# Turning the neighbour mask of a graph network: TensorE transposes replaced by DMA transposes, and 22 masks split 11 and 11 instead of 14 and 8

## The chip, the cores and the metric

The kernel runs on one core of a Trainium2 chip. Its time is the device time of one execution in microseconds, as the median of several runs. Beside it there is one execution recorded by the profiler, and all durations of single instructions come from that one.

## The reference

A graph has N = 2708 nodes with D = 512 numbers each and an adjacency matrix `adj` of N x N integers (0 or 1, some 2.4% ones, the diagonal all ones). Four layers follow each other, each with a residual sum and a layer norm. Only the first uses a limited mask: of each row's neighbours it keeps the first 64.

```python
def _L0_gnn_ref(X, A, W_nb, b_nb, W_line, b_line, neibor_num):
    Ab = A > 0
    keep = Ab & (jnp.cumsum(Ab.astype(jnp.int32), axis=1) <= neibor_num)
    cnt = keep.sum(axis=1, keepdims=True).astype(X.dtype)
    nb_sum = keep.astype(X.dtype) @ X
    nb_mean = nb_sum / jnp.maximum(cnt, 1.0)
    xj = jax.nn.leaky_relu(nb_mean @ W_nb.T + b_nb)
    xi = jax.nn.leaky_relu(X @ W_line.T + b_line)
    return xi + jnp.where(cnt > 0, xj, jnp.zeros((), X.dtype))
...
x = _layernorm(x + _L0_gnn_ref(x, adj, L0_gnn_W_nb, L0_gnn_b_nb, L0_gnn_W_line, L0_gnn_b_line, 64), axis=-1)
x = _layernorm(x + _L1_gnn_ref(x, adj, ...), axis=-1)
x = _layernorm(x + _L2_gnn_ref(x, adj, L2_gnn_W, L2_gnn_a), axis=-1)
x = _layernorm(x + _L3_gnn_ref(x, adj, ...), axis=-1)
```

Layer 1 averages over all neighbours, layers 2 and 3 are graph attention with the same adjacency as a mask.

## The kernel before

The rows are cut into NT = 22 tiles of P = 128 (the last has 20 rows, `few`). TensorE contracts over the partitions, so each aggregation over neighbours needs the mask with its *columns* on the partitions: `maskT` (L82) is 128 x 22 x 2816 in fp8; `maskT[p, j, i]` tells of node i and its neighbour j x 128 + p. It stays in SBUF for all four layers. It holds three values: a neighbour that is kept is negative, one beyond the 64th positive, no neighbour is zero. What comes after the first layer takes the sign off.

**How one mask (one tile of 128 rows of `adj`) is made.**

1. `load_mask` (L270) brings 128 x 2708 integers from memory as bf16 on POOL's DMA queue.
2. `count` (L275): ScalarE turns it into exact 0 and 1 (Sigmoid with a huge scale) and sums each row into `cnts`.
3. `place` (L279): DVE runs a scan along the row (L283), a running sum from -64.5, capped at 0.5, then multiplies the mask by it (L286). A neighbour thus gets its negative place or a positive half. A row is done in 2 parts in the first stage and in 4 among the sums.
4. `turn` (L288): TensorE transposes 22 blocks of 128 x 128 in bf16 (L295) into PSUM, in three groups of at most G = 8; after each group ScalarE takes the Sign from PSUM to `maskT` (L299), which also changes bf16 to fp8. After the last group a small DMA on POOL's queue (L302) copies the 20 rows of the last block to partitions 32 to 51 (`TWIN`), where the low half of y's last tile lies.

The masks are made in the order `turns` (L268): the short cut of tiles 20 and 21 first, so mask 1 is the one with 20 rows.

**First stage** (L331 to L358), one pass over the 22 row tiles. Each row t has two products of 512 x 512 on TensorE: y = x W_nb^T (L335) and xi = x W_line^T (L350). `transposed` (L129) turns x by TensorE (L133), and ScalarE copies it out of PSUM (`xT`, L135). `keep_y` (L230) keeps y in two parts, the rounded `yH` on ScalarE (L231) and the remainder `yL` on DVE (L236). DVE adds the bias and applies the leaky relu (L352, L195), and POOL's queue stores xi to `r0_dram` (L354). Rows of x are loaded two ahead on SP's queue (`fetched`, L171), into three row buffers. In this pass HERE = NT - 8 = 14 masks are made, one at a row where the condition in L343 holds: two out of three rows or more, from row 2 on. A mask is loaded one mask ahead (`early(1, ...)`, L326, three buffers `m`). At its row it is counted after `yH` (L346), placed in two parts after `yL` and after the leaky relu (L348, L356), and turned about one row later (L339).

The order on an engine is largely the order in which the code issues; `pe` (L104) chains TensorE's instructions one after another by hand, and `tc.issue_after` holds an instruction behind a named one.

**Sums** (L483 to L510). Six cuts of up to four row tiles, the short one first. For each j of 22 column tiles, ScalarE makes `kT` (L369), the kept mask as 0 or 1 in fp32r, from `maskT`, one step ahead, and TensorE does 8 matmuls of 128 x 512 (4 tiles, `yH` and `yL`) into four PSUM banks (L496). At the end of a cut ScalarE evicts the four sums (L509). At each j the loop also advances a generator `both` by one step (L502): first `other_masks` (L372), which makes the other 8 masks, one each 11 steps or so, in time for their cut; then `weights1` and `vectors`, which prepare the weights of later layers. Another generator, `todo`, advanced two times out of three, is `finish` (L410): the last cut's leaky relu, residual sum and layer norm on DVE, and its store on POOL's queue. The mask's buffers there are `room(i)` (L374), two of them by turns; the transposes use the PSUM tiles `pm0`, `pm1` (L397). `weight2` (L211) holds W_line in the first stage and again a weight from `weights1` on; in between it is not used.

What follows (L515 on) is layer 1's products, its aggregation over `maskT` and the attention layers, 2445 of the 2924 us. It is the same in both kernels.

Of the kernel before, what the change touches and what calls it, by code (L numbers as in the profile page):

```python
# [11 lines left out]
BF16 = mybir.dt.bfloat16  # L12
F8 = mybir.dt.float8e4
AF = mybir.ActivationFunctionType
# [4 lines left out]
P = 128  # L19
# [7 lines left out]
STEP = 2.0 ** 68  # L27
# [3 lines left out]
def kernel(  # L31
# [9 lines left out]
    nc = tc.nc  # L41
    N = x.shape[0]
    NT = -(-N // P)
    FULL = N // P
# [5 lines left out]
    def rows(t):  # L50
        return min(P, N - t * P)
# [11 lines left out]
    identb = const.tile([P, P], BF16, name="identb")  # L63
    nc.vector.tensor_copy(identb, ident)
    G = 8
# [16 lines left out]
    maskT = big.tile([P, NT, NT * P], F8, name="maskT")  # L82
# [12 lines left out]
    few = N - (NT - 1) * P  # L95
    LAST, TWIN = NT - 1, 32
# [61 lines left out]
    def early(first, n, make):  # L158

        made = {}  # L160

        def get(i, **how):
            for j in range(len(made), min(i + first + 1, n)):
                made[j] = make(j, **how)
            return made[i]
        return get
# [36 lines left out]
    with ExitStack() as phase:  # L203
        yp = phase.enter_context(tc.tile_pool(name="y", bufs=1))
        cnts = yp.tile([P, NT], F32, name="cnts")
# [56 lines left out]

        HERE = NT - 8
        cuts = [(b, min(b + 4, NT)) for b in range(0, NT, 4)]
        cuts = cuts[-1:] + cuts[:-1]
        turns = [t for b in cuts for t in range(*b)]  # L268

        def load_mask(i, m):  # L270
            n = rows(turns[i])
            nc.gpsimd.dma_start(m[:n], adj[turns[i] * P:turns[i] * P + n, :], max_dma_last_dim=N * 2)
            return m

        def count(i, m):  # L275
            t, n = turns[i], rows(turns[i])
            nc.scalar.activation(m[:n], m[:n], AF.Sigmoid, bias=gate[:n], scale=STEP, accum_out=cnts[:n, t:t + 1])

        def place(i, m, places, part, of):  # L279

# [4 lines left out]
                                         OP.add, OP.min)  # L285
            return nc.vector.tensor_mul(m[:n, c0:c1], m[:n, c0:c1], places[:n, :c1 - c0])  # L286

        def turn(i, m, psum, order=as_it_comes):  # L288
            t, n = turns[i], rows(turns[i])
            for g0 in range(0, NT, G):  # L290
                g1 = min(g0 + G, NT)
                ps = psum()
                for j in range(g0, g1):
                    w = rows(j)
                    order(nc.tensor.transpose(ps[:w, j - g0, :n], m[:n, j * P:j * P + w], identb[:n, :n]))  # L295
                parts = [(P, g0, min(g1, FULL))] + ([(rows(FULL), FULL, NT)] if g1 > FULL else [])
                for w, a, b in parts:
                    if a < b:
                        nc.scalar.activation(maskT[:w, a:b, t * P:t * P + n], ps[:w, a - g0:b - g0, :n], AF.Sign,  # L299
                                             saturate=False)  # L300
                if g1 == NT:
                    nc.gpsimd.dma_start(maskT[TWIN:TWIN + few, LAST, t * P:t * P + n],  # L302
                                        maskT[:few, LAST, t * P:t * P + n])
                yield

        def rows_of(src):
            return early(2, NT, lambda t: fetched(src, t, rows(t)))

        with ExitStack() as ph:
            st = ph.enter_context(tc.tile_pool(name="l0a", bufs=1))  # L310
            wnT, wlT = weight(), weight2
            room = [maskT[:, G + k, :4 * D].bitcast(F32) for k in range(2 * KD)]

            xs = rows_of(x)
            xTs = early(0, NT, lambda t, order=as_it_comes: transposed(ahead, ps_tr, xs(t), rows(t), "xT", order))

            transpose_weight(room[:KD], ps_tr, wnT, l0_w_nb, (nc.sync, nc.scalar))
            lows = {}  # L320
            for t in range(2):
                xT = xTs(t, order=pe)
                lows[t] = keep_y(t, P, product(xT, P, wnT, 0, pe))
            transpose_weight(room[KD:], ps_tr, wlT, l0_w_line)
            b_line = bias(bcast(l0_b_line, D))
            masks = early(1, HERE, lambda i: load_mask(i, st.tile([P, N], BF16, name="m", bufs=3)))  # L326
            masks(0)
            nc.gpsimd.memset(maskT[:, NT - 1, :], 0.0)
            nc.gpsimd.memset(maskT[:, :, N:], 0.0)
            counted = turned = 0  # L330
            for t in range(NT):  # L331
                n = rows(t)
                if t > 1:

                    lows[t] = keep_y(t, n, product(xTs(t, order=pe), n, wnT, 0, pe, sums() if t % 2 else None))  # L335
                xT = xTs(t)
                if t + 1 < NT:
                    xTs(t + 1, order=pe)
                while turned < counted - (t + 2 < NT):  # L339
                    for _ in turn(turned, masks(turned), lambda: sums(BF16, (P, G, P)), pe):  # L340
                        pass
                    turned += 1
                now = counted < min(HERE, -(-(t - 1) * HERE // (NT - 5)))  # L343
                if now:
                    m, places = masks(counted), st.tile([P, N // 2], BF16, name="places", bufs=1)
                    with tc.issue_after(highs[t].ins):  # L346
                        count(counted, m)
                    with tc.issue_after(lows[t].ins):  # L348
                        place(counted, m, places, 0, 2)
                pm = product(xT, n, wlT, 1, pe)  # L350
                u = sm.tile([P, D], F32, name="u")
                nc.vector.tensor_add(u[:n], pm[:n], b_line[:n])  # L352
                low = rows_made = leaky(u[:n], u[:n])
                nc.gpsimd.dma_start(r0_dram[t * P:t * P + n, :], u[:n])  # L354
                if now:
                    with tc.issue_after(low.ins):  # L356
                        place(counted, m, places, 1, 2)
                    counted += 1  # L358
# [3 lines left out]
        with ExitStack() as ph:  # L362
# [9 lines left out]
            def other_masks():  # L372

                def room(i):  # L374
                    r = (ahead.tile([P, 2 * KD * (D + 2 * H)], BF16, name="w", tag="w", bufs=1) if i % 2 else
                         st.tile([P, 2 * KD * D], BF16, name="spare", tag="spare"))
                    m = r[:, :N]
                    load_mask(i, m)
                    return m, r[:, N:N + N // 4 + 1]

                got = {HERE: room(HERE)}
                for i in range(HERE, NT):
                    if i + 1 < NT:
                        got[i + 1] = room(i + 1)
                    m, places = got.pop(i)
                    if i == HERE:
                        for _ in range(5):
                            yield
                    count(i, m)
                    yield  # L390
                    yield
                    for part in range(4):
                        place(i, m, places, part, 4)
                        yield
                    yield
                    yield
                    psum = (ps_mm.tile([P, G, P], BF16, name=f"pm{k % 2}") for k in range(3))  # L397
                    for _ in turn(i, m, lambda: next(psum)):
                        yield
                nc.vector.tensor_scalar(iso, cnts, 0.5, None, op0=OP.is_lt)  # L400
                nc.vector.tensor_scalar(rdeg, cnts, 1.0, None, op0=OP.max)
                nc.vector.reciprocal(rdeg, rdeg)
# [83 lines left out]
            for i, b in enumerate(cuts):  # L486
                ts_ = range(*b)
                pa = {t: sums() for t in ts_}
                for j in range(NT):
                    if j + 1 < NT:  # L490
                        nxt, nxt_made = kept(b, j + 1)
                    elif i + 1 < len(cuts):
                        nxt, nxt_made = kept(cuts[i + 1], 0)
                    for t in ts_:
                        for y in halves(j):
                            nc.tensor.matmul(pa[t], kT[:, (t - b[0]) * P:(t - b[0] + 1) * P], y[:, j, :],  # L496
                                             start=(j == 0 and y is yH), stop=(j == LAST))
                    kT = nxt
                    if j % 3:
                        next(todo, None)  # L500
                    with tc.issue_after(nxt_made.ins):
                        next(both, None)  # L502
                with tc.issue_after(nxt_made.ins):
                    reciprocals(slice(*b))
                us = {}
                for t in ts_:
                    n = rows(t)
                    us[t] = st.tile([P, D], F32, name=f"u{t - b[0]}")
                    nc.scalar.activation(us[t][:n], pa[t][:n], AF.Copy, scale=rkeep[:n, t:t + 1])  # L509
                todo = finish(ts_, us)  # L510
# [6 lines left out]
            for t in range(NT):  # L517
                n = rows(t)
# [989 lines left out]
```

## Time and profile before

| | us |
|---|---|
| runs | 2923.65, 2928.71, 2920.36 |
| median | 2923.65 |
| profiled execution, its own time | 2926.44 |
| its span, first to last instruction | 2924.5 |
| first stage and what lies ahead of it, to the first matmul of the sums | 202.5 |
| sums, to the last eviction | 276.7 |
| all the rest | 2445.3 |

Over the whole span TensorE is busy 2842.8 us (97%), its weight loads 1584.3, DVE 1983.5 (68%), ScalarE 1499.8 (51%), POOL 244.8 (8%). By stage:

| stretch | length | TensorE | DVE | ScalarE | POOL | share of the DMA engines |
|---|---|---|---|---|---|---|
| to the first sum | 202.5 | 187.7 | 152.8 | 95.9 | 36.6 | 0.50 |
| sums | 276.7 | 269.8 | 162.4 | 136.7 | 33.9 | 0.39 |
| rest | 2445.3 | 2385.3 | 1668.2 | 1267.2 | 174.3 | 0.17 |

The table's shares are means over a stretch; the engine that decides can change inside it. Matmuls are pipelined, so TensorE's busy time includes time in which one waits in the pipe.

In the groups of the profile a line reads: source line, engine, operation, output <- input by the program's names, shape and type, count; then busy time and mean ns of one, and the engine's idle time before such an instruction with what ended it. In a timeline a line begins with the start and the duration in us. In the list of DMA issues the numbers are the count, the KB of each and the median time from issue to landing.

### The profile page before, as it was taken

The page shows a single profiled execution, that of the slowest core. Times are in us where ns is not written, and L with a number is a line of the kernel's source. Part 1 is how long each engine was busy: PE and PEld are TensorE (multiplying, and loading weights), DVE is VectorE, ACT ScalarE, POOL GpSimd, SP SyncE. Part 2 cuts the span into 40 slices and gives each one's busy share as a digit, 9 for nine tenths or more (in the row PEclk, how much of TensorE's full clock was granted, in tenths as well). Part 3 has the DMA queues.
Part 4 walks back from the last instruction along what each step waited for, and adds up shares of the span by engine and source line. Part 5 has one row for each costly group of instructions (what it writes and reads, how often), then busy time and mean ns, then how long its engine had stood idle before and what let it go on. Part 6 is the DMA issues. An engine that isn't in the chain of part 4 may idle for free. (4 is left out here: it accounts for less than half of the span.)

```text
span 2924.5 us, 36470 instructions
## 1 busy us (share of the span) xinstructions
PE 2842.8 (97%) x14370; PEld 1584.3 (54%) x14370; DVE 1983.5 (68%) x2341; ACT 1499.8 (51%) x1749; POOL 244.8 (8%) x387
## 2 busy tenths in 40 slices
PE   8999999999999999999999999999999999999997
PEld 4557766458888333444466443444375555555555
DVE  6866637542334999999978999999954435435342
ACT  3546532112322999999965999999951000000001
POOL 1111101101110000000012000000200010100000
PEclk9999999999999999999999999999999999999999
DMA  5633426322222111111143111110161000000000
GB/s 130 131 88 72 109 80 184 123 63 91 83 72 78 33 37 36 35 45 39 38 142 122 37 37 36 45 51 34 35 160 60 4 26 15 26 15 16 15 22 21
DMA packets 122518, 181.58 MB, mean 62 GB/s; under 512 B 43007, under 2 KB 67908, under 8 KB 122338
## 3 DMA queue, kind: packets, MB, share of 16 engines
q1 hardware_dynamic: 92470, 117.50, 13.5%
q0 software_dynamic: 18864, 57.45, 6.9%
q10 hardware_dynamic: 11004, 4.22, 0.6%
q8 instruction: 115, 1.88, 0.3%
q14 instruction: 65, 0.53, 0.1%
HBM read 148.91 MB, written 44.65 MB: 66 GB/s over the span
## 5 line engine op out<-in xcount | busy, mean ns | idle before, releaser
L752 DVE SCALAR_TENSOR_TENSOR e<-v_bc,ucol,maskT 128x1408 f32<-128x1408 f32 (+3 forms) x804 | 1133.7, 1477 | 322.3 <-PE pn L1135 312.8
L781 ACT ACTIVATE c<-e,bcol 128x1300 fp8e4<-128x1300 f32 (+2 forms) x688 | 956.6, 1412 | 63.4 <-DVE e L752 18.6
L953 PE MATMUL po<-e,R 128*64 128x512 f32 (+3 forms) x4224 | 894.7, 548 | 26.3 <-DVE e L752 24.3
L953 PEld LDWEIGHTS po<-e,R 128*64 128x64 f32 (+1 forms) x4224 | 333.4, 136 | 554.7 <-issue 390.4
L1135 PE MATMUL pn<-e,R 128*128 128x512 f32 (+3 forms) x1056 | 403.0, 545 | 1.1 <-DVE lin L1155 0.3
L1135 PEld LDWEIGHTS pn<-e,R 128*128 128x128 f32 (+1 forms) x1056 | 183.9, 190 | 197.1 <-issue 181.5
L1085 ACT ACTIVATE w<-pl,b 128x256 f32<-128x256 f32 (+1 forms) x88 | 40.9, 465 | 371.0 <-PE pl L1083 371.0
L496 PE MATMUL acc<-yH,kT 128*128 128x512 f32 x484 | 195.2, 409 | 4.7 <-ACT kT L369 4.5
L547 PE MATMUL acc<-yH,mf 128*128 128x512 f32 x484 | 185.0, 389 | 0.0
L496 PE MATMUL acc<-yL,kT 128*128 128x512 f32 x462 | 180.8, 391 | 0.0
L547 PE MATMUL acc<-yL,mf 128*128 128x512 f32 x462 | 179.7, 389 | 0.0
L122 POOL TENSOR_TENSOR ln_rs<-ln_rs,half 128x1 f32<-128x1 f32 (+1 forms) x88 | 53.0, 602 | 1397.7 <-DVE ln_rs L121 1348.4
L674 PE MATMUL pm<-w,xT 128*128 128x264 f32 (+1 forms) x704 | 165.1, 387 | 3.4 <-ACT xT L135 1.6
L259 PE MATMUL pm<-weight,xT 128*128 128x512 f32 (+1 forms) x344 | 158.4, 604 | 8.2 <-DVE u L352 6.8
L1083 PE MATMUL pl<-lin 128*128 128x256 f32 (+1 forms) x704 | 155.9, 376 | 3.4 <-DVE lin L982 3.4
L1108 PE MATMUL pl<-lin,w 128*128 128x512 f32 x336 | 150.8, 593 | 0.0
L1083 PEld LDWEIGHTS pl<-lin 128*128 128x128 f32 x704 | 131.2, 193 | 34.5 <-issue 15.8
L674 PEld LDWEIGHTS pm<-w,xT 128*128 128x128 f32 (+1 forms) x704 | 129.7, 190 | 25.8 <-ACT xT L135 3.6
L544 ACT CAST mf<-maskT 128x1024 fp32r<-128x1024 fp8e4 (+1 forms) x66 | 64.5, 978 | 151.7 <-PE acc L547 148.1
L259 PE MATMUL pm<-w,xT 128*128 128x512 f32 x296 | 133.6, 594 | 5.8 <-ACT xT L135 2.1
L369 ACT ACTIVATE kT<-maskT 128x512 fp32r<-128x512 fp8e4 (+1 forms) x132 | 77.5, 594 | 115.6 <-PE acc L496 114.4
L853 PE MATMUL pd<-c,parts_c 128*12 128x384 fp8e4 (+2 forms) x2688 | 128.3, 307 | 0.0
(251 smaller groups left out, 2656.2 us busy)
## 6 DMA issues: line engine op xcount, KB each, us to landing
rows<-x_dram SPq DMA_DIRECT2D x63, 256.0 KB
v_bc<-v_dram SPq DMA_DIRECT2D x16, 704.0 KB
rows<-in_x_dram SPq DMA_DIRECT2D x42, 256.0 KB
x_dram<-u POOLq DMA_DIRECT2D x42, 256.0 KB, 2.5
v_bc<-v_dram SPq DMA_DIRECT2D x16, 650.0 KB
m<-in_adj_dram POOLq DMA_DIRECT2D x13, 677.0 KB, 6.9
r_dram<-u POOLq DMA_DIRECT2D x21, 256.0 KB, 2.3
rows<-r_dram SPq DMA_DIRECT2D x21, 256.0 KB
```

The lines of the kernel that those rows point to most:

```text
L259: order(nc.tensor.matmul(pm[:m], xT[:, k, :m], w[:, k, :], start=(k == 0), stop=(k == KD - 1)))
L369: made = nc.scalar.activation(kT[:, :w], maskT[:, j, b[0] * P:b[0] * P + w], AF.Relu, scale=-1.0)
L496: nc.tensor.matmul(pa[t], kT[:, (t - b[0]) * P:(t - b[0] + 1) * P], y[:, j, :], start=(j == 0 and y is yH), stop=(j == LAST))
L547: nc.tensor.matmul(pa, mf[:, j - g0, :], y[:, j, :], start=(j == 0 and y is yH), stop=(j == LAST))
L674: nc.tensor.matmul(pm[a][:m, :D // 2 + heads], xT[:, k, :m], w[:, k, a, :D // 2 + heads], start=(k == 0), stop=(k == KD - 1))
L752: self.made = nc.vector.scalar_tensor_tensor(e[:, :w], v[:, :w], ucol[:, j, h:h + 1], maskT[:, j, c0:c0 + w], op0=OP.max, op1=OP.mult)
L781: nc.scalar.activation(c[:, :w], e[:, :w], AF.Sigmoid, bias=bcol[:, j, h:h + 1], scale=STEP, saturate=False)
L853: pe(nc.tensor.matmul(p[32 * g:32 * g + 12, :c1 - c0], parts_c[:, j, h, :], c[:, c0:c1], start=(i == 0 and h == hs[0]), stop=(i == NT - 1 ...
L953: pe(nc.tensor.matmul(po[i][HO * k:HO * k + HO, :c1 - c0], R2[at, j, h * HO:(h + 1) * HO], e[at, a:a + c1 - c0], start=(i_ == 0), stop=(i_ ...
L1083: nc.tensor.matmul(pl[:, :w], self.lin1[:, k, f * P:(f + 1) * P], h[:, k, :w], start=(k == 0), stop=(k == KD - 1))
L1108: nc.tensor.matmul(pl[:n], gT[:, f, (t - t0) * P:(t - t0) * P + n], self.lin2[:, f, :], start=(f == 0), stop=(f == KF - 1))
L1135: nc.tensor.matmul(pn[k][:, :w], R2[at, j, k * P:(k + 1) * P], e[at, :w], start=(j == 0), stop=(j == NT - 1))
```

## The change

It does four things.

- **The turn.** The 22 TensorE transposes of a mask are replaced by one DMA transpose of the whole tile, 128 x 2816 in bf16, issued on SP's queue (`nc.sync.dma_start_transpose`). It writes 22 blocks of 128 x 128 into a buffer `into` in SBUF. A new generator `signs` does what ScalarE did before, from `into` instead of PSUM: Signs of 8, 8 and 5 blocks and of the 20 rows of the last block, then the small copy on POOL's queue.
- **Where the turned mask lands.** In the first stage there are four slots `idle`, pairs of column tiles of `maskT` whose own masks are not made yet, seen as bf16, taken by turns. Among the sums there is one buffer, `weight2` seen as bf16.
- **Its input.** The mask tiles are widened from 2708 to 2816 columns, and POOL zeroes the 108 spare ones before each load (the whole tile for the short mask).
- **The split.** HERE is NT - 11: eleven masks in the first stage, eleven among the sums. There `both` is advanced four steps for each three j, `signs` of the last mask runs between the parts of the next one's `place`, and the steps after a turn are three.

In the first stage, the Signs of a mask are issued just ahead of the next mask's transpose, about one row and a half after its own.

```diff
-        HERE = NT - 8
+        HERE = NT - 11
...
-            nc.gpsimd.dma_start(m[:n], adj[turns[i] * P:turns[i] * P + n, :], max_dma_last_dim=N * 2)
+            nc.gpsimd.dma_start(m[:n, :N], adj[turns[i] * P:turns[i] * P + n, :], max_dma_last_dim=N * 2)
...
-        def turn(i, m, psum, order=as_it_comes):
+        def turn(i, m, into):
+            nc.sync.dma_start_transpose(into, m)
+
+        def signs(i, into):
             t, n = turns[i], rows(turns[i])
-            for g0 in range(0, NT, G):
-                g1 = min(g0 + G, NT)
-                ps = psum()
-                for j in range(g0, g1):
-                    w = rows(j)
-                    order(nc.tensor.transpose(ps[:w, j - g0, :n], m[:n, j * P:j * P + w], identb[:n, :n]))
...
+            for w, a, b in [(P, a, min(a + G, FULL)) for a in range(0, FULL, G)] + [(few, FULL, NT)]:
+                nc.scalar.activation(maskT[:w, a:b, t * P:t * P + n], into[:w, a:b, :n], AF.Sign, saturate=False)
                 yield
+            nc.gpsimd.dma_start(maskT[TWIN:TWIN + few, LAST, t * P:t * P + n],
+                                maskT[:few, LAST, t * P:t * P + n])
...
-            masks = early(1, HERE, lambda i: load_mask(i, st.tile([P, N], BF16, name="m", bufs=3)))
+            idle = [maskT[:, :, (HERE - 1 + 2 * i) * P:(HERE + 1 + 2 * i) * P].bitcast(BF16) for i in range(4)]
+
+            def mask_rows(i):
+                m = st.tile([P, NT * P], BF16, name="m", bufs=3)
+                nc.gpsimd.memset(m[:, N:], 0.0)
+                if rows(turns[i]) < P:
+                    nc.gpsimd.memset(m, 0.0)
+                return load_mask(i, m)
+
+            masks = early(1, HERE, mask_rows)
...
                 while turned < counted - (t + 2 < NT):
-                    for _ in turn(turned, masks(turned), lambda: sums(BF16, (P, G, P)), pe):
+                    for _ in signs(turned - 1, idle[(turned - 1) % 4]) if turned else ():
                         pass
+                    turn(turned, masks(turned), idle[turned % 4])
                     turned += 1
+                if t + 1 == NT:
+                    for _ in signs(turned - 1, idle[(turned - 1) % 4]):
+                        pass
...
-                    m = r[:, :N]
+                    m = r[:, :NT * P]
+                    nc.gpsimd.memset(m[:, N:], 0.0)
                     load_mask(i, m)
-                    return m, r[:, N:N + N // 4 + 1]
+                    return m, r[:, NT * P:NT * P + N // 4 + 1]
 
-                got = {HERE: room(HERE)}
+                got, left = {HERE: room(HERE)}, iter(())
+                into = weight2.rearrange("p k c -> p (k c)").bitcast(BF16)[:, :NT * P].rearrange("p (t n) -> p t n", n=P)
...
                     for part in range(4):
                         place(i, m, places, part, 4)
+                        next(left, None)
                         yield
+                    for _ in left:
+                        pass
                     yield
                     yield
-                    psum = (ps_mm.tile([P, G, P], BF16, name=f"pm{k % 2}") for k in range(3))
-                    for _ in turn(i, m, lambda: next(psum)):
-                        yield
+                    turn(i, m, into)
+                    left = signs(i, into)
+                    yield
+                    yield
+                    yield
+                for _ in left:
+                    yield
...
-                        next(both, None)
+                        for _ in range(1 + (j % 3 == 0)):
+                            next(both, None)
```

## The prediction

> **What bounds the kernel now.** I read the page, then the busy time of the engines in stretches of the first stage, then DVE's, ScalarE's and TensorE's timelines where mask rows lie, then the groups by line, then the DMA issues. In the first stage two engines take turns. The columns after the stretch are its length and the busy time of PE, PEld, DVE, ACT and POOL:
>
> ```profile
> 40.00:60.00 20.00, 18.59 (x86) 9.42 (x85) 19.86 (x18) 10.50 (x14) 2.34 (x4) 1.00 0.37 87
> 120.00:140.00 20.00, 18.68 (x87) 9.92 (x86) 19.86 (x19) 10.72 (x17) 4.15 (x7) 1.00 0.64 130
> ```
>
> Where every row tile carries a mask, DVE is full (19.86 of 20 us) and PE nearly so. DVE's own timeline has the price of a mask row:
>
> ```profile
> 47.54 0.85 DVE L286 TENSOR_TENSOR m<-m,places 128x1354 bf16<-128x1354 bf16 x1
> ...
> 111.73 2.97 DVE L283 TENSOR_TENSOR_SCAN places<-m,over 128x1354 bf16<-128x1354 bf16 x1
> 114.74 0.87 DVE L286 TENSOR_TENSOR m<-m,places 128x1354 bf16<-128x1354 bf16 x1
> ...
> 121.29 2.97 DVE L283 TENSOR_TENSOR_SCAN places<-m,over 128x1354 bf16<-128x1354 bf16 x1
> ...
> 129.47 0.86 DVE L286 TENSOR_TENSOR m<-m,places 128x1354 bf16<-128x1354 bf16 x1
> ```
>
> From the first scan of one mask to the first scan of the next is 9.56 us, and two masks in a row take 111.73 to 130.33, so 18.6 us. PE needs less for a row: two products of 3.43 us (eight records 0.43 us apart), four turns of x at 0.11 us, 7.3 us in all, and 1.4 us more where a mask is turned on it. The stage ends so:
>
> ```profile
> 193.91 1.50 PE L295 MATMUL acc<-identb,m 128*128 128x128 bf16 x22
> 195.34 3.70 PE L259 MATMUL pm<-weight,xT 128*128 128x512 f32 x8
> 198.97 3.64 PE L259 MATMUL acc<-w,xT 128*52 128x512 f32 x8
> 202.54 0.50 PE L496 MATMUL acc<-yH,kT 128*128 128x512 f32 x1
> ```
>
> The sums then run on PE, four row tiles to a cut. ScalarE's evictions mark the cuts:
>
> ```profile
> 276.20 1.25 ACT L509 ACTIVATE u<-acc,rkeep 128x512 f32<-128x512 f32 x2
> ...
> 320.49 1.83 ACT L509 ACTIVATE u<-acc,rkeep 128x512 f32<-128x512 f32 x3
> ...
> 364.80 1.83 ACT L509 ACTIVATE u<-acc,rkeep 128x512 f32<-128x512 f32 x3
> ```
>
> A cut with two masks lasts 44.3 us. Its 172 matmuls at 0.227 us make 39.1, PE idles some 0.5 us, so a mask turned here costs PE (44.3 - 39.1 - 0.5) / 2 = 2.35 us.
>
> **The change in the first stage.** The change takes 22 x 22 turns off PE: 14 masks x 1.4 us = 20 us here, and it moves three masks (23 us of DVE) to the sums. It puts a DMA transpose of 128 x 2816 bf16, 721 KB, on SP's queue, then four Signs a mask that read SBUF. I cost the Signs at no more than before: the group from PSUM has 1.0 us for 128 x 1024, the copy that reads maskT in SBUF has 978 ns for the same size.
>
> What decides is where the first Sign stands. In the changed program's order ScalarE has, for each pair of masks a and b in neighbouring rows: count a, yH, xT, count b, first Sign of a, yH, xT, the other Signs of a, first Sign of b, yH, xT, count of the next a. The first Sign waits for its transpose, and behind it wait the yH and xT copies of the next row, which the next product on PE waits for, and the next count, which DVE's next scan waits for. So the stage becomes a ring: count a 2.7 us (2.55 and the gap to the scan), DVE on a and b 18.6, the transpose of b, which I call D, first Sign 1.0, yH and xT 1.2, and again: 23.5 + D for three rows and two masks. PE's 22 us for three rows lie beneath. Eleven masks at rows 2, 3, 5, 6 and so on give five such periods after mask 0. Mask 0 is placed at 48.4 us (47.54 + 0.85), as now, so the last mask's first Sign runs at 48.4 + D + 5 x (23.5 + D) = 165.9 + 6D. From there to the first sum: Sign and copies 2.2, three products 10.3 and a turn of x 0.5, 13.0. First sum at 178.9 + 6D against 202.5: **-23.6 + 6D us**.
>
> **What D is.** The trace has no DMA transpose. The rows that bear on it:
>
> ```profile
> oT_dram<-oT POOLq DMA_DIRECT2D x4, 704.0 KB, 4.1
> m<-in_adj_dram POOLq DMA_DIRECT2D x13, 677.0 KB, 6.9
> x_dram<-u POOLq DMA_DIRECT2D x42, 256.0 KB, 2.5
> q10 hardware_dynamic: 11004, 4.22, 0.6%
> ```
>
> Below: a third of the bytes lands in 2.5 us, and I take that as the low end. As many bytes in long rows land in 4.1. The mask load, to the same partitions, takes 6.9. The small packets of the last row (0.38 KB each) cost 0.6% x 16 x 2924.5 / 11004 = 25.5 ns of one of 16 engines: 2816 pieces of 128 numbers make 4.5 us, and with the 1.6 us in which the shortest copy of maskT lands, 6.1. If it moves 16 numbers at a time, 22528 such pieces are 35.9 us, the high end. I take **D = 6**, between the mask load and the long rows and equal to the count by pieces. First stage: -23.6 + 36 = +12.4.
>
> The Trainium skill speaks against the change: VectorE: DVE Perf Modes, in its section The three transpose paths, gives a 128 x 128 bf16 block 1309 ns by DMA and 390 ns on TensorE, where this trace has 56 to 66 ns (1.2 to 1.5 us for 22). An estimate by that page, 22 x 1.309, would be D = 28.8 and a first stage of +149 us. Advanced Engine Details and Errata, section X-Bar Transpose (TRN2), says the opposite, that such transposes run like ordinary DMAs at 350 to 400 GB/s; its estimate, 2 us and the latency of 1.6, would be D = 3.6 and -2 us. Neither enters the sum.
>
> **The sums.** Eight masks leave PE: 8 x 2.35 = -18.8. Three more masks' counts and Signs come to ScalarE, 3 x (2.7 + 2.8) = 16.5 us, which hold up the kT copies that PE needs; a copy's lead of about one step (1.8 us in a long cut) hides a part, so 0 to 16.5, and I take +13, since the first cut has steps of only 0.9 us, and holds two of the masks. The transpose has a cover: by the generator's steps, at 4/3 of a step to each j, the first Sign of mask i stands five steps, 3.75 j, after its transpose; that is 6.7 us in a cut of four tiles and 3.4 in the short one, 6.1 on average. DVE takes some of it: a cut has 22 x 8 / 66 = 2.67 masks of 8.6 us (four scans of 1.62, four products of 0.52) and four finishes of 4.3, together 40.2, where PE has 39.1. With 1.2 us late, the cover is 4.9, and 11 masks wait D - 4.9 each: 11 x 1.1 = +12.1. Sums: -18.8 + 13 + 12.1 = **+6.3**.
>
> **Edits that I cost at nothing.** POOL's zeroing of the 108 spare columns (a 128 x 2376 zeroing took 2.1 us, so 0.1 to 0.3 each) stands before the mask load, and now waits for the transpose that frees the buffer; behind it are r0's stores and the few-row copies, which nothing awaits soon, and the load still lands a row before its count. Without that cover it is 0.3 x 11. The short mask's whole zeroing, at most 5 us, is early, before 30 us, and its count comes at 46. On SP the row loads stand behind transposes; they are fetched two rows ahead, and SP now waits 184 us for PE's release of the row buffers, so a queue held for D shows only when D passes a row, 7.3 us.
>
> Total at D = 6: 12.4 + 6.3 = +18.7. The profiled run took 2926.4 (span 2924.5 and 1.9 around it), 2.8 over the median; its sum is 2945.1, and against the median 2923.65 it is **2942 us**.
>
> **The rivals.** In all, the change is T(D) = -29.4 + 6D + 11 max(0, D - 4.9).
> 1. The wait at the Sign outweighs the work taken off PE (forecast): D from 5.4 to 8.5, +9 to +61 us. For it: the DVE-full rows, so nothing else can fill ScalarE's wait. Against it: two of the rows put D below 5. 0.47.
> 2. Faster: the transpose lands so early that the ring goes round at 23.5 + D with D below 3.4, and PE's 39 us are worth having. At D = 2.5 it is -14 us, 2909. It decides from D = 3.4, where T is -9. For it: the 2.5 us row, and both ends in SBUF. Against it: three times its bytes, and loads that share the rings (DMA share 0.37 to 0.64). 0.13.
> 3. Balance: D from 3.4 to 5.4, T within 9 us; the 4.1 us row gives -5, 2919. 0.22.
> 4. A slow transpose, in small pieces, which holds SP's queue as well, so that x is late too: D above 8.5. At D = 12 T is +121, 3045; at 35.9 it is +527. For it: the packet prices grow with pieces, not bytes. Against it: no row of this size takes over 9 us. 0.18.
>
> That PE is not relieved at all is excluded: the program's order has no mask turns on PE.
>
> **How the numbers follow.** Something like 9 us (0.3%) is about what a measurement of this kernel tells from no change. Slower is cases 1 and 4, 0.65; same is case 3, 0.22; faster is case 2, 0.13. Time: case 1 at D = 6. Its own range is 2932 to 2985. The range for 8 in 10 reaches into case 2 as far as D = 3 (-11) and into case 4 as far as D = 10.5 (+95): 2912 to 3020; about 0.1 lies below and above each.
>
> **What would show it.** After the change: DMA waits in front of ScalarE's Signs, some 6 to 11 us long on every second mask of the first stage, DVE under 19 of 20 us there, the first sum at 179 + 6D; six us more on the stage for each us of D. In the sums no mask turns on PE, cuts of about 44 us in spite of it. I am wrong if the Signs find their data there, if D is below 3.4, or if DVE is still full in the mask rows.

## The result and the profile after

The changed kernel takes 2956.91 us (median of four runs, 2956.34 to 2959.76) against 2923.48: ratio 1.0114, 95% interval 1.0097 to 1.0132. It is slower by 33.4 us. The two profiles differ by 30.0 us, and by stages (the sums are taken here to the start of the very last eviction, 1.5 us later than in the table ahead of the prediction):

| stretch | before | after | difference | forecast |
|---|---|---|---|---|
| to the first matmul of the sums | 202.5 | 230.7 | +28.2 | +12.4 |
| sums, to the start of the last eviction | 278.2 | 289.8 | +11.6 | +6.3 |
| rest | 2443.8 | 2434.0 | -9.8 | 0 |

The rest is the same code. In the fourteen profiles of this study it took between 2434.0 and 2446.2 us, so a difference of this size between two single profiles says nothing of the change.

The engines in stretches of the changed kernel's first stage (length, then PE, PEld, DVE, ACT, POOL busy, granted clock, share of the DMA engines, GB/s), for the two stretches shown of before:

```profile
40.00:60.00 20.00, 17.13 (x45) 7.59 (x44) 17.86 (x14) 8.87 (x11) 2.00 (x4) 1.00 0.37 82
120.00:140.00 20.00, 14.19 (x37) 6.19 (x37) 10.64 (x14) 8.00 (x11) 3.40 (x7) 0.93 0.89 172
```

DVE, full before (19.86), stands for half of the second stretch; PE stands too, and the DMA engines' share has risen from 0.64 to 0.89. ScalarE's timeline over one period of two masks tells why (start, duration, instruction; in brackets the idle time before it and its releaser):

```profile
107.06 2.56 ACT L277 ACTIVATE m<-m,gate 128x2708 bf16<-128x2708 bf16 x1
...
114.99 2.55 ACT L277 ACTIVATE m<-m,gate 128x2708 bf16<-128x2708 bf16 x1
117.44 0.19 ACT L277 ACTIVATION_READ_ACCUMULATOR m<-m,gate 128x1 f32 x1
123.85 1.06 ACT L294 ACTIVATE maskT<-maskT 128x1024 fp8e4<-128x1024 bf16 x1 [6.22 <-DMA maskT<-m]
...
135.78 2.00 ACT L294 ACTIVATE maskT<-maskT 128x1024 fp8e4<-128x1024 bf16 x2 [8.15 <-DMA maskT<-m]
137.69 0.57 ACT L231 CAST yH<-acc 128x512 fp32r<-128x512 f32 x1
138.15 0.59 ACT L135 COPY xT<-ps_tr 128x512 f32<-128x512 f32 x1
138.63 2.56 ACT L277 ACTIVATE m<-m,gate 128x2708 bf16<-128x2708 bf16 x1
```

The first Sign of a mask waits for its transpose, and behind it stand yH and xT of the next row and the next count. From one count to the count two masks later it is 31.6 us. The view of what ScalarE waited for in the first stage has the sum, in us, times, longest:

```profile
ACT maskT L294 <- DMA maskT<-m: 90.2, 11, 12.1
```

PE waits in turn for the copies of x that stand behind these Signs, from 40 us on:

```profile
PE pm L259 <- ACT xT L135: 16.5, 4, 5.8
PE acc L259 <- ACT xT L135: 12.9, 2, 8.3
```

Before, PE had no wait for xT in this stretch.

DVE's scans stand still with it. In its timeline the first scans of two masks and of the next one:

```profile
109.74 2.98 DVE L283 TENSOR_TENSOR_SCAN places<-m,over 128x1354 bf16<-128x1354 bf16 x1 [1.74 <-ACT m L277]
...
118.61 2.98 DVE L283 TENSOR_TENSOR_SCAN places<-m,over 128x1354 bf16<-128x1354 bf16 x1
...
141.32 2.98 DVE L283 TENSOR_TENSOR_SCAN places<-m,over 128x1354 bf16<-128x1354 bf16 x1 [1.74 <-ACT m L277]
```

8.9 us between two masks of a pair, then 22.7 to the next. Two neighbouring transposes are not alike. SP's queue (a transpose's duration there is the time it held the queue) and POOL's:

```profile
118.65 3.31 SPq L289 DMA_TRANSPOSE maskT<-m  x1
122.06 0.53 SPq L173 DMA_DIRECT2D rows<-in_x_dram  x1
127.48 5.23 SPq L289 DMA_TRANSPOSE maskT<-m  x1
```

```profile
89.34 0.19 POOL L323 MEMSET m<- 128x108 bf16 x1 [8.88 <-DMA maskT<-m]
89.83 0.72 POOL L272 DMA_DIRECT2D m<-in_adj_dram  x1 [0.29 <-issue]
...
124.50 0.74 POOL L272 DMA_DIRECT2D m<-in_adj_dram  x1
```

The first was followed by its Sign after 5.20 us, the second, beside which the load of a mask ran, after 8.30. The load comes there because POOL zeroes and loads a buffer only once a transpose has set it free: at 89.34 it had waited 8.88 us for the first transpose of a pair, and the load then ran beside the second, issued at 93.33. (At 124.50 a store that had waited for DVE came free at the same moment.)

Among the sums the evictions mark the cuts:

```profile
269.55 1.25 ACT L525 ACTIVATE u<-acc,rkeep 128x512 f32<-128x512 f32 x2
...
311.68 2.40 ACT L525 ACTIVATE u<-acc,rkeep 128x512 f32<-128x512 f32 x4
...
360.82 2.41 ACT L525 ACTIVATE u<-acc,rkeep 128x512 f32<-128x512 f32 x4
```

The short cut takes 38.8 us (30.0 before), then 42.1 and 49.1, where before had 43.6 and 44.3, although no mask turn is left on PE.

### The profile page after: what moved, and what is told of

Its sections match the earlier page's. It is cut to its first block, busy times and chain, and to the rows that moved or that the text cites. A ratio compares the mean times of both kernels' runs of the same rounds, so it can differ in the third digit from the quotient of the medians.

```text
span 2954.5 us, 35601 instructions
## 1 busy us (share of the span) xinstructions
PE 2830.8 (96%) x13886; PEld 1565.7 (53%) x13886; DVE 1984.0 (67%) x2353; ACT 1501.5 (51%) x1749; POOL 251.2 (9%) x410
## 5 line engine op out<-in xcount | busy, mean ns | idle before, releaser
L768 DVE SCALAR_TENSOR_TENSOR e<-v_bc,ucol,maskT 128x1408 f32<-128x1408 f32 (+3 forms) x804 | 1133.8, 1474 | 318.0 <-PE pn L1151 310.8
L797 ACT ACTIVATE c<-e,bcol 128x1300 fp8e4<-128x1300 f32 (+2 forms) x688 | 956.7, 1412 | 61.1 <-DVE e L768 15.8
L259 PE MATMUL pm<-w,xT 128*128 128x512 f32 x296 | 143.5, 630 | 19.6 <-ACT xT L135 18.6
L1099 PEld LDWEIGHTS pl<-lin 128*128 128x128 f32 x704 | 130.4, 192 | 34.3 <-issue 15.8
```

Of the source, the lines that this page charges most:

```text
L259: order(nc.tensor.matmul(pm[:m], xT[:, k, :m], w[:, k, :], start=(k == 0), stop=(k == KD - 1)))
L768: self.made = nc.vector.scalar_tensor_tensor(e[:, :w], v[:, :w], ucol[:, j, h:h + 1], maskT[:, j, c0:c0 + w], op0=OP.max, op1=OP.mult)
L797: nc.scalar.activation(c[:, :w], e[:, :w], AF.Sigmoid, bias=bcol[:, j, h:h + 1], scale=STEP, saturate=False)
L1099: nc.tensor.matmul(pl[:, :w], self.lin1[:, k, f * P:(f + 1) * P], h[:, k, :w], start=(k == 0), stop=(k == KD - 1))
```

## The experiments

In the twelve kernels below, the first sum is the start of the first matmul of the sums, and the sums' length is up to the start of the last eviction, both from the one profiled execution. The kernel before had medians of 2927.5 to 2927.9 us beside them.

**late3: the Signs wait elsewhere.** The Signs of a mask counted at row t are held behind a named instruction, yH of row t + 3.

```diff
...
-                    for _ in signs(turned - 1, idle[(turned - 1) % 4]) if turned else ():
-                        pass
                     turn(turned, masks(turned), idle[turned % 4])
                     turned += 1
-                if t + 1 == NT:
-                    for _ in signs(turned - 1, idle[(turned - 1) % 4]):
-                        pass
+                while signed < turned and (at[signed] + 3 <= t or t + 1 == NT):
+                    with tc.issue_after(highs[t].ins):
+                        for _ in signs(signed, idle[signed % 4]):
+                            pass
+                    signed += 1
...
+                    at.append(t)
...
```

> The Signs of a mask counted at row t are held behind yH of row t+3, nothing else is changed. Theory (the wait at the first Sign sets the stage): the DMA waits in front of the Signs go from 90 us to under 10 us; a period of three rows falls from 31.7 us (71.99 to 198.65 in four periods) to the 22 us that TensorE needs for them, five periods give 48 us back, so the first sum comes at 182 to 195 us and the median at 2909 to 2921 us. Rival 1 (row loads of x queued behind transposes on SP hold the rows): ScalarE no longer waits, but TensorE waits for xT behind late rows; first sum at 215 us or later, median over 2940. Rival 2 (the lower granted clock, 0.74 to 0.93 in these slices, sets the stage, not the wait): the clock stays low and the first sum is over 215 us.

Measured: median 2921.05 us, ratio to before 0.9973 (0.9961 to 0.9986), so 36 us under the changed kernel (40 if each is set against the runs of the kernel before that stood beside it). First sum 197.2, sums 291.5. What ScalarE waited for from 40 us to the first sum, and PE's wait for xT:

```profile
ACT yH L231 <- PE acc L259: 34.0, 9, 8.2
ACT yH L231 <- PE pm L259: 28.9, 7, 6.8
ACT maskT L294 <- DMA maskT<-m: 11.9, 3, 8.8
```

```profile
PE acc L259 <- ACT xT L135: 2.7, 1, 2.7
```

Now ScalarE waits for PE, as an engine that isn't the bound should. The waits at the Signs fell from 90.2 to 11.9 us, PE's for xT from 29.4 to 2.7 and the first stage by 33.5, with every transpose, load and Sign still there: the theory stands and both rivals fall. The first sum is 2 us later than its range. Four later kernels with this same first stage had it at 185.1, 191.4, 191.4 and 189.8, so it differs from run to run; the runs of this kernel lie between 2915.75 and 2927.84.

**noload: what makes the second transpose long.**

```diff
-                return load_mask(i, m)
+                if i < 3:
+                    return load_mask(i, m)
+                nc.gpsimd.memset(m[:, :N], 1.0)
+                return m
```

> The changed kernel, but masks 3 to 10 of the first stage are not loaded: POOL fills them with ones. Theory (a mask's load that runs beside the second transpose of a pair makes it 7.6 to 11.8 us long, where the first takes 5.3): all transposes of the first stage take 5 to 6 us from issue to the first Sign, and the first sum comes at 169 + 6 x 5.5 = 202 us. Rival (row loads of x, or the order of the two transposes, do it): the second ones stay at 7.5 us or more, first sum over 215 us.

Measured: one run, 2951.32 us; the kernel leaves out the loads of eight masks. SP's queue, and ScalarE's first Sign after the second of these transposes:

```profile
79.35 3.84 SPq L289 DMA_TRANSPOSE maskT<-m  x1
...
88.68 3.36 SPq L289 DMA_TRANSPOSE maskT<-m  x1
```

```profile
94.33 1.06 ACT L294 ACTIVATE maskT<-maskT 128x1024 fp8e4<-128x1024 bf16 x1 [6.03 <-DMA maskT<-m]
```

All eleven now take 5.2 to 6.3 us from issue to the first Sign; the load beside them was the cause. In the changed kernel itself the second transpose of the last pair, when no mask of this stage was left to load, took 5.9. The second ones are still a little longer (5.6 to 6.3, against 5.2 to 5.3 for the first), which no run explains. The first sum came at 216.5 us, not 202: the expectation left out the 13 us that lie between the last mask's first Sign and the first sum. With them, and mask 0's transpose at 50.7 us where the forecast had 48.4, the ring gives 165.9 + 2.3 + 35.5 (the six transposes that count) + 13 = 216.7.

**nl3: both together** (late3 with the edit of noload).

> The kernel with the Signs held back three rows (late3), but masks 3 to 10 of the first stage are not loaded: POOL fills them with ones. Theory (in late3 the DMA engines are the next bound: their share is 0.85 to 1.22 from 60 to 160 us, and a transpose stands 8 to 10 us on SP): transposes stand 3.3 to 4 us on SP, no DMA waits at the Signs, first sum at 182 to 191 us, where late3 has 197.2. Rival (TensorE and DVE set late3's stage as it is): first sum at 195 us or later.

Measured: one run, 2915.99 us, first sum 184.3. The same stretch (140 to 160 us) of late3 and then of nl3:

```profile
140.00:160.00 20.00, 15.15 (x42) 6.79 (x40) 11.98 (x10) 8.26 (x12) 3.06 (x6) 1.00 1.22 161
```

```profile
140.00:160.00 20.00, 18.47 (x50) 8.54 (x49) 17.40 (x19) 12.25 (x16) 3.56 (x7) 1.00 0.60 139
```

Without the loads the DMA share falls from 1.22 to 0.60 and PE goes from 15.15 to 18.47 us busy. (The share adds up the time of packets, so it can pass 1.) So in this pair of profiles the loads' traffic is what is left once the Signs are out of the way. How much it is worth isn't shown: nl3 is one run, and the same first stage with the loads came between 185.1 and 197.2 us.

**d14late3: the old split with DMA transposes and late Signs.** The edit of late3, HERE = NT - 8, the slots from column tile 12 on, and one step of the generator for each j.

> DMA transposes with the old split (14 and 8 masks, one step of the generator for each j) and the Signs held behind yH three rows after the count. Theory: the first stage is set by DVE again (two thirds or more of its rows with a mask, 9.3 us each), first sum 190 to 202 us; the sums lose 8 x 2.35 us of TensorE's turns and take back little, 10 to 18 us shorter than before; median 2893 to 2912 us. Rival (the transposes' traffic itself slows rows and sums, wherever the Signs stand): not faster than 2920 us.

Measured: median 2914.14 us, ratio 0.9965 (0.9944 to 0.9986). The ten runs fall into two groups, 2909 to 2918 and 2931 to 2934, and the profiled one, 2930.62, belongs to the second. The median lies 2 us above the theory's range. Its sums are 266.6 us, as expected; its first sum is at 223.3, not 190 to 202. SP's and POOL's queues there:

```profile
88.56 13.30 SPq L289 DMA_TRANSPOSE maskT<-m  x1
101.96 1.01 SPq L173 DMA_DIRECT2D rows<-in_x_dram  x2
103.07 14.97 SPq L289 DMA_TRANSPOSE maskT<-m  x1
```

```profile
88.82 0.72 POOL L272 DMA_DIRECT2D m<-in_adj_dram  x1 [0.29 <-issue]
...
116.43 0.19 POOL L323 MEMSET m<- 128x108 bf16 x1 [25.81 <-DMA maskT<-m]
```

The transpose issued at 88.56, beside a mask's load and with the rows of x behind it, was done only by 116.4, some 28 us later, and PE stood for 13.0 us of that time. It wasn't held by the Sign: PE waited for DVE, and DVE 13.7 us for a store of xi that POOL had issued at 90.05. From 92 to 112 us the DMA share was 1.27 while only 63 GB/s were moved. So the rival had a part in this profile: with 14 masks the traffic held the stage. That the other two runs over 2930 us are of the same kind isn't shown, since one run was profiled.

**pe11: the new split alone.** The kernel before with HERE = NT - 11 and the four steps for three j; TensorE turns all masks.

> The kernel before with only the new split (11 masks in the first stage, 11 among the sums, four steps of the generator for three j); masks are turned by TensorE as before. It tells the move of three masks from the new way of turning. Theory (the move takes DVE's load off the first stage and puts 3 x 2.35 us of TensorE and up to 16.5 us of ScalarE on the sums): first stage 5 to 23 us shorter, sums 7 to 28 us longer, median 2915 to 2945 us. Rival (the 11.6 us that the changed kernel's sums are longer come from the transposes' waits alone): sums within 10 us of the kernel before.

Measured: median 2941.2 us, ratio 1.0042 (1.0028 to 1.0056). First sum 193.3 (9.2 earlier), sums 310.8 (32.6 longer, above the range). So the move alone costs some 13 us. Against it the sums of the changed kernel, with the DMA transposes, are 310.8 - 289.8 = 21 us shorter.

**sumdma: the new turn only among the sums.** The kernel before with `signs` and the DMA transposes in `other_masks`, and nothing else.

```diff
...
+        def turn_dma(i, m, into):
+            nc.sync.dma_start_transpose(into, m)
...
-                    psum = (ps_mm.tile([P, G, P], BF16, name=f"pm{k % 2}") for k in range(3))
-                    for _ in turn(i, m, lambda: next(psum)):
-                        yield
+                    turn_dma(i, m, into)
+                    left = signs(i, into)
+                    yield
+                    yield
+                    yield
...
```

> The kernel before, with only the eight masks among the sums turned by DMA (one step of the generator for each j, as before); the first stage keeps TensorE's turns and its 14 masks. Theory (among the sums, where the DMA engines have room, the new turn pays: 8 x 2.35 us off TensorE against a few waits): first sum within 2 us of 202.5, sums 264 to 270 us against 278.2, ratio 0.995 to 0.998. Rival (the gain in the sums of d14late3 came from work that its long first stage had already done): sums 275 us or more, ratio 0.999 or more.

Measured: median 2909.01 us, ratio 0.9935 (0.9923 to 0.9947), the fastest of the kernels that do the whole work, and better than the ratio expected. First sum 202.9, sums 267.3, both as the theory has them. Its evictions:

```profile
233.34 1.25 ACT L529 ACTIVATE u<-acc,rkeep 128x512 f32<-128x512 f32 x2
...
274.53 2.37 ACT L529 ACTIVATE u<-acc,rkeep 128x512 f32<-128x512 f32 x4
...
315.87 2.37 ACT L529 ACTIVATE u<-acc,rkeep 128x512 f32<-128x512 f32 x4
```

41.2 and 41.3 us a cut, where before had 43.6 and 44.3. By the profiles the stages account for 10.5 us of a gain of 17.8; the other 7.3 lie in the rest. They can't be put down to the edit: the rest took 2436.5 us here and 2446.2 in mix2 below, which has the same steps among the sums.

**l3sl and l3fcsl: when the Signs come among the sums.** In l3sl, on top of late3:

```diff
...
                         place(i, m, places, part, 4)
-                        next(left, None)
+                        if part > 1:
+                            next(left, None)
                         yield
+                    next(left, None)
+                    yield
                     for _ in left:
                         pass
                     yield
-                    yield
...
```

> late3 with the Signs among the sums two steps of the generator later: two of the four stand at the third and fourth part of the next mask's place, the others in the step after it. Theory (the Signs' waits for their transposes, 16 us in all, hold kT and so TensorE): these waits under 5 us, sums 280 to 286 us against late3's 291.5, median 2910 to 2916 us. Rival (what is long among the sums is ScalarE's own work, counts and Signs of eleven masks between the kT copies, and the waits are hidden): sums 288 to 293 us, median within 4 us of 2921.

Measured: median 2916.89 us, ratio 0.9963 (0.995 to 0.9976); sums 289.7, first sum 185.1. The Signs still wait 11.4 us for transposes, and the sums are as long as late3's 291.5 within 2 us: nearer to the rival. The lower median can't be put down to this edit, since the first stage, which it doesn't touch, was 12 us shorter in this profile.

l3fcsl has besides `range(1 + (j % 3 == 0 and i > 0))`.

> As l3sl, and in the first, short cut the generator is advanced once for each j instead of four times for three. Theory (in the short cut a step of TensorE is 0.92 us, shorter than one Sign, so every piece of a mask's work on ScalarE stops TensorE there): the short cut 30 to 35 us against 39.5, the later cuts together no longer than in l3sl, median 2905 to 2912 us. Rival (the work is only moved to later cuts): sums within 2 us of those of l3sl.

Measured: median 2918.77 us, ratio 0.9965 (0.9953 to 0.9977). The short cut falls to 29.7 us from 37.6, as the theory has it, but the sums take 290.0: the rival is right, the work is only moved.

**nocount and noplace: which part of a mask is long among the sums.** On top of l3sl, nocount drops `count(i, m)` and noplace drops `place(i, m, places, part, 4)` there.

> l3sl without the counts of the eleven masks among the sums (cnts stays 1 for these rows, the masks themselves are already 0 and 1). Theory (a count, 2.74 us on ScalarE with its read, is longer than the one step of 1.8 us by which kT leads, so each stops TensorE): about 11 x (2.74 + 0.6 - 1.8) = 17 us less, sums 268 to 277 us against l3sl's 289.7. Rival (DVE sets the cuts with three masks, 3 x 8.6 + 4 x 4.3 = 43 us): sums 284 us or more.

> l3sl without the scans and products on DVE among the sums, so the masks of these rows are not limited to 64 places and their signs are not turned; counts, transposes and Signs remain. Theory (ScalarE's counts and Signs are what is long): sums 284 us or more. Rival (DVE sets the cuts with three masks): sums 266 to 277 us.

Measured: nocount one run, 2919.53 us, sums 291.0; noplace one run, 2903.8 us, sums 275.0. Both times the rival is right. The cut with three masks, in l3sl and then in noplace (length, PE, PEld, DVE, ACT, POOL):

```profile
264.40:311.90 47.50, 41.23 (x174) 31.59 (x172) 39.87 (x59) 30.95 (x46) 10.29 (x16) 0.99 0.63 144
```

```profile
263.20:306.40 43.20, 40.89 (x174) 31.69 (x172) 15.71 (x35) 30.96 (x45) 8.89 (x16) 1.00 0.73 163
```

ScalarE's busy time is the same in both, DVE's falls by 24.2 us and the cut by 4.3. Without the counts nothing that shows is gained, while the waits at the Signs rise from 11.4 to 19.1 us; without DVE's part the sums are 14.7 us shorter over all cuts, and the Signs wait 2.8 us. DVE isn't full in this cut (39.87 of 47.5). How it acts there can be read in l3sl, on SP's queue and on ScalarE:

```profile
302.88 3.35 SPq L289 DMA_TRANSPOSE weight<-w  x1
```

```profile
308.08 1.06 ACT L294 ACTIVATE maskT<-weight 128x1024 fp8e4<-128x1024 bf16 x1 [4.74 <-DMA weight<-w]
309.04 0.61 ACT L377 ACTIVATE kT<-maskT 128x512 fp32r<-128x512 fp8e4 x1
```

DVE's last product of this mask ends at 302.74 and the transpose follows at once. Its first Sign waits 4.74 us for it, the next kT stands behind the Sign, and PE waits 3.46 us for that kT: most of the 4.3. So in this cut DVE acts by making a transpose late. For the other cuts this isn't shown.

**sd13 and mix2: is there something better than sumdma?** sd13 is sumdma with HERE = NT - 9.

> As sumdma (TensorE's turns in the first stage, DMA transposes among the sums, one step of the generator for each j), with 13 and 9 masks. Theory (what a mask costs among the sums goes by how densely they stand: at one step for each j there are two to a cut, DVE 2 x 8.6 + 4 x 4.3 = 34 us of a cut's 40): sums 264 to 270 us as with eight masks, first sum 197 to 201 us, ratio to before 0.990 to 0.9935. Rival (each mask more costs the 7.7 us that lie between 8 and 11 masks, 266.6 and 289.7): sums 273 us or more, ratio 0.9935 or more.

Measured: median 2914.87 us, ratio 0.9957 (0.9943 to 0.9971). First sum 199.4; sums 271.7, between the two ranges: a ninth mask costs 4.4 us there and gives 3.5 back in these two profiles. The ratio is the rival's, and the kernel isn't faster than sumdma.

mix2 is d14late3 with this in the first stage:

```diff
...
-                    turn(turned, masks(turned), idle[turned % 4])
+                    if turned % 2:
+                        turn(turned, masks(turned), idle[turned % 4])
+                    else:
+                        for _ in turn_pe(turned, masks(turned), lambda: sums(BF16, (P, G, P)), pe):
+                            pass
...
```

> 14 and 8 masks; in the first stage every second mask by DMA transpose with its Signs held behind yH three rows after the count, the others by TensorE; among the sums by DMA. Theory (the DMA engines were full in d14late3 because all 14 masks went through them; half of them fit, and 7 x 1.4 us leave TensorE where it and DVE are both nearly full): DMA share under 0.95 in the slices of the stage, first sum 195 to 200 us, ratio to before 0.990 to 0.993. Rival (with 14 masks DVE alone sets the stage): first sum 200.5 to 204 us, ratio as sumdma's, 0.9935.

Measured: median 2913.91 us, ratio 0.9946 (0.9926 to 0.9965); first sum 204.4, sums 266.3. From 40 us on the DMA share stayed at 0.92 or less, and yet the first stage didn't get shorter: the rival is right, though the first sum is 0.4 us beyond its range. With 14 masks, time taken from PE there is worth nothing that this profile shows.

## Why the prediction was right, and where it was wrong

The forecast was the case that came: slower, because the wait at the Sign outweighs what PE is spared, and the time lies in that case's own range. Its size was some 15 us short. By the profiles it was further off than that: the two stages grew by 39.8 us where the sum had 18.7, and the rest, for which the sum had nothing, was 9.8 us shorter. That the total came as near as it did is in part luck.

- **The ring.** Counts of the first mask of a pair stand at 71.99, 107.06, 138.63, 169.50 and 198.65 us. The periods are 35.1, 31.6, 30.9 and 29.2; 23.5 + D with the second transposes' 11.82, 8.30, 7.60 and 5.88 gives 35.3, 31.8, 31.1 and 29.4. The last mask's first Sign was to run at 165.9 us and six D; the six (with mask 1's 9.74 and the last mask's 5.59) sum to 48.9, so 214.8, and it ran at 215.79. late3 shows that it is this wait, and not the transposes as such.
- **The term that was mis-sized: D = 6.** For a transpose by itself it was good: 5.2 us. The count by pieces holds: the packets of the hardware queue rose by 62656, 2848 for each of 22 transposes, and their time by some 22 ns each. But in the ring the second of each pair counts, and these had a mean of 8.15 with the last. 2.15 x 6 = 12.9 us, and 3.0 because mask 0's transpose was issued at 51.4 and not at 48.4 us (it lies between 48.4 and 51.4 in the profiles of kernels with eleven masks turned by DMA there), make 15.9; the first stage was missed by 15.8. The sum had one D for all transposes and no term for a load beside one.

The two queue lines, before and then after (packets, MB, share of 16 engines):

```profile
q1 hardware_dynamic: 92470, 117.50, 13.5%
```

```profile
q1 hardware_dynamic: 155126, 133.36, 16.3%
```

- **The edit costed at nothing that wasn't free.** The mask's load, behind POOL's wait for the transpose, was said to land in time, and it did: no count of the first stage waited for it. That it would then run beside the next transpose and stretch it wasn't seen. noload puts it at 14.2 us of the first stage. The 184 us that SP was said to wait for PE's release of the row buffers were misread: by the trace before, 136.4 us of SP's waits in this stage are for PE's turns of x. Nothing else rests on them.
- **The sums.** For eight masks the sum was good, since -18.8 and eight waits of 1.1 make -10.0 and sumdma has -10.9; but not term by term. ScalarE waited 3.0 us at sumdma's Signs and not 8.8, and what took the other 5 us isn't shown. The +13 for three masks more was too small: from sumdma to the changed kernel's sums it is 22.5 us, of which 3.3 were in the waits' term. The path was the one that the prediction has, a kT that comes late for PE. What PE waited for kT among the sums, in us, times, longest, before, in sumdma and in the changed kernel:

```profile
PE acc L496 <- ACT kT L369: 4.5, 7, 1.7
```

```profile
PE acc L516 <- ACT kT L380: 6.1, 9, 1.7
```

```profile
PE acc L511 <- ACT kT L375: 20.5, 16, 5.1
```

That is 14.4 of the 22.5 us, and ScalarE's waits at the Signs went from 3.0 to 16.2 us with it. The cause was another than the one given: taking out the counts (nocount) gained nothing, taking out DVE's scans and products (noplace) gained 14.7 us. So it was less ScalarE's own work than transposes that DVE sets off late. The Signs were not taken out by themselves, and the other 8 us are not accounted for.

- **The rivals.** The faster case would have needed D under 3.4; no transpose here was followed by its Sign in under 5.1. The case of a slow transpose, above 8.5, came for single transposes only (9.7 and 11.8 here, 28 in d14late3's profile), and not because of small pieces: each transpose is 2848 packets in all. The argument for that case, that packets are priced by pieces and not by bytes, doesn't come out of the rows before either: q1's packets of 1.27 KB took 68 ns each, the 0.38 KB ones 25.5. SP's queue, held for 3.3 us and more by each transpose, cost nothing seen in the first stage: in late3 it was held as long or longer.
- **What was to be seen.** Waits of 6 to 11 us stood at every mask's Sign, not only at every second one (5.7 to 12.1); DVE was under 19 of 20 us in the mask rows; the first sum followed 179 + 6D, 227.8 against 230.7.

The two estimates by the Trainium skill stood far apart: 28.8 us by VectorE: DVE Perf Modes, section The three transpose paths, and 3.6 us by Advanced Engine Details and Errata, section X-Bar Transpose (TRN2). The measured 5.2 us of a transpose by itself is nearer to the second; 5.2 / 22 is 0.24 us a block, against the 1.309 that the first page gives for one block. For a transpose beside a load the measured 7.6 to 11.8 us decide.

## What to carry to other kernels

Ask of every new wait what is queued behind it on its engine: here a Sign at the head of ScalarE's queue cost 33 us of a stage, and holding it back to three rows after the count, with nothing taken out, gave them back. A transfer that takes the place of engine work must be costed beside the transfers that it sets off, not by itself. And a part of a change that pays can be looked for alone: the same transposes, put only where the DMA engines and the order leave room, gave a kernel 0.65% faster than before, of which the two stages account for a little over half.

## What the runs showed of the hardware that was not expected

A DMA transpose of 128 x 2816 bf16 holds SP's queue for 3.3 us and has its first reader 5.2 us after its issue when alone; beside the load of a mask that was 7.6 to 11.8 us, and once, in d14late3, some 28.

When PE had stood for some microseconds, its next product was slow. PE's timeline in the changed kernel:

```profile
107.22 6.76 PE L259 MATMUL acc<-w,xT 128*128 128x512 f32 x8 [8.35 <-ACT xT L135]
113.81 0.60 PE L133 MATMUL ps_tr<-ident,rows 128*128 128x128 f32 x4
114.25 3.60 PE L259 MATMUL pm<-weight,xT 128*128 128x512 f32 x8
```

After 8.35 us of idling eight matmuls take 6.76 us, the next eight 3.60, and the granted clock of that stretch (100 to 120 us) is 0.74. It cost nothing that shows here, since DVE's 18.6 us for two masks ran beside it: in the ring above there is no place for it, and the periods fit within 0.3 us without it. The Trainium skill's TensorE: Matmul & The Clock Gate, section Part 1: The HAM clock gate, states that the clock is halved after at least one idle window of about 3.4 us and comes back after at least one busy window of that length. Here the granted clock falls to 0.50 at about 103 us, some 4 us after PE stopped, and is back at 1.00 at about 113.4, some 6 us after PE started again. That agrees with the page, but the return takes longer than one window.
